# A four-layer kernel on a 256x256x128 image: how layer 1 is loaded, stored and summed

## The chip, the cores and the metric

The kernel runs on one core of a Trainium2 chip. The metric is the device time of one execution in microseconds. The engines of the core are TensorE (PE, with its weight loads shown apart as PEld), VectorE (DVE), ScalarE (ACT), GpSimd (POOL) and SyncE (SP). SP, ACT and POOL can issue DMAs; SP and ACT do it through the hardware queues, POOL through a software queue. All of them are carried out by the core's 16 DMA engines.

## The reference, cut to what matters

The input is x, 256 x 256 positions by 128 channels, in float32. Four layers each add to x what they compute from a group-normalised x. Layer 0 is an attention along rows with a bias between pairs of positions; layers 2 and 3 are not touched by the change. Layer 1 is what the change is about: two sets of 16 planes a and b of 256 x 256, a matrix product of each pair of planes, a normalisation over the 16 channels, and a gate.

```python
def _gn(v, G=32, eps=1e-5):            # per group of 4 channels, over all positions
    ...
def _L1_conv_ref(x, Wa1, ba1, Wa2, ba2, Wb1, bb1, Wb2, bb2, ln2_g, ln2_b, Wg, bg, Wz, bz):
    a = jax.nn.sigmoid((x @ Wa1 + ba1) * (x @ Wa2 + ba2))      # 16 channels
    b = jax.nn.sigmoid((x @ Wb1 + bb1) * (x @ Wb2 + bb2))
    g = jax.nn.sigmoid(x @ Wg + bg)
    z = jnp.einsum('bikc,bkjc->bijc', a, b)                    # one product of planes a channel
    return g * (_ln(z, ln2_g, ln2_b) @ Wz + bz)

x = x + _L0_conv_ref(_gn(x), ...)      # attention
x = x + _L1_conv_ref(_gn(x), ...)
x = x + _L2_conv_ref(_gn(x), ...)
x = x + _L3_conv_ref(_gn(x), ...)
```

## The kernel before

The image is kept in device memory with channels as rows: x1T is x after layer 0 (128 rows of 65536 positions, 32 MB), x2T is x after layer 1. It is worked on in 32 pieces of 2048 positions (SC), 1 MB each; NSC is 32, CK is 512.

Layer 0 first writes the transposed input xT and collects moments; then, in an order of pieces given by a list, it computes the bias of pairs and the sums of squares. Pieces in `held` are resident and are written out by keep(), the others are fetched:

```python
fresh = range(RES - 3, RES)
order = list(range(RES - 3, RES + 4))
for i in range(RES - 3):
    order += [i, RES + 4 + i] if RES + 4 + i < NSC else [i]
# ... in the loop over order:
if s not in held:
    fetch()
    if i > 1:
        keep()
```

The setup of the attention turns the bias (tri) and multiplies it with the row scales, one head at a time, in one DVE instruction:

```python
rsT = eb.tile([P, 2, N], F32, name="p2_rsT", tag="p2_es", bufs=5)
nc.scalar.copy(rsT, pt)
# ...
def turn_pair(h):
    pt = psM.tile([P, 2, N], F32, name="p2i_t", tag="p2_mm")
    turn(pt, tri[:, h, :, :])
    nc.vector.scalar_tensor_tensor(triT[:, h, :, :], pt, toff[:, h : h + 1], rsT, ALU.add, ALU.mult)
```

The attention works on 64 groups of 1024 positions and stores each to x1T on SP's queue. Each half group adds an entry to the statistics (stats1, 128 entries). After it a flag is computed from an aggregate of these statistics (a fallback is taken if something isn't finite), and only then do the folds of layer 1 begin, with a second aggregate of the same statistics (gn_finish):

```python
mv = sb.tile([P, 2], F32, name="chk_mv")
nc.vector.bn_aggr(mv, stats1.rearrange("p n s -> p (n s)"))
# ... flag
again = nc.values_load(flag[0:1, 0:1], min_val=0, max_val=1)
with tc.If(again > 0):
    general_attention(...)
layer0.close()
m1, r1 = gn_finish(stats1, "gn1")
# ... folds of the weights: v1, v2, vb1, vb2, wgf, bgf
```

Layer 1, the a/b stage: each piece is loaded, multiplied with the two sets of weights (a and b side by side: 32 rows for each quarter of the piece, 128 partitions in all), and stored as 32 rows of abD. Eight pieces stay resident for the gate stage.

```python
def store_groups(queue, dst, s, src):
    queue.dma_start(dst[:, s * SC : (s + 1) * SC].rearrange("c (q t) -> q c t", q=4), src)

held = {s: xres.tile([P, SC], F32, name=f"x1_{s}") for s in range(0, NSC, NSC // R1)}   # R1 = 8
for s in range(NSC):
    xt = held[s] if s in held else xsb.tile([P, SC], F32, name="p3_x", tag="xs")        # 3 buffers
    nc.sync.dma_start(xt, x1T[:, ss])
    # ... 8 matmuls into p1 and p2
    s1 = sb.tile([P, CK], F32, name="p3_s1")
    nc.scalar.activation(s1, p1, AF.Identity, bias=vb1)
    nc.vector.scalar_tensor_tensor(s1, p2, vb2, s1, ALU.add, ALU.mult)
    ab = sb.tile([P, CK], F32, name="p3_ab", bufs=10)
    nc.scalar.activation(ab, s1, AF.Sigmoid)
    store_groups(nc.gpsimd, abD, s, ab)
```

The product: 16 pairs of planes, loaded by four, turned, multiplied. The sum and the sum of squares over the channels are kept on POOL, and at the end each plane is scaled with the inverse deviation and stored to znD.

```python
nc.vector.tensor_tensor(Z[:, k, :], pz, base, ALU.subtract)
nc.scalar.activation(sq, Z[:, k, :], AF.Square)
nc.gpsimd.tensor_tensor(s1, s1, Z[:, k, :], ALU.add)
nc.gpsimd.tensor_tensor(s2, s2, sq, ALU.add)
# ... after the last plane:
for i in range(3):
    fetch1(xsb, "xs", 3)                      # pieces for the gate stage
# ... s1 = 1 / sqrt(s2 / 16 - (s1 / 16)^2 + eps)
for q in range(4):
    zq = Z[:, 4 * q : 4 * q + 4, :]
    nc.vector.tensor_tensor(zq, zq, s1.unsqueeze(1).to_broadcast([P, 4, 2 * N]), ALU.mult)
    nc.sync.dma_start(znD[4 * q : 4 * q + 4, :].rearrange("c (p t) -> p c t", p=P), zq)
```

The gate stage takes the pieces once more, with the planes znD in blocks of four pieces, and writes x2T:

```python
zns[b] = sb.tile([P, 4, CK], F32, name="p4_zn", bufs=3)          # fetch_zn(b): 4 loads on SP
# per piece: 4 matmuls with wgf, 2 sigmoids (ACT), 4 matmuls of planes,
# 2 scalar_tensor_tensor (DVE), then
nc.gpsimd.tensor_tensor(xt, xt, gt, ALU.add)
# finish: 4 bn_stats (DVE), store of the piece to x2T on SP; then the next fetch1
# into "xs" (3 buffers) or "xs2" (4 buffers)
```

Of the kernel before, what the change touches and what calls it, by code (L numbers as in the profile page):

```python
# [32 lines left out]
def kernel(ctx: ExitStack, tc: tile.TileContext, a: dict, out: bass.AP):  # L33
# [169 lines left out]
    def gn_groups(mv, name):  # L203
        with tc.tile_pool(name=name + "_ps", bufs=1, space=PSUM) as ps, tc.tile_pool(
# [4 lines left out]
            mean = const.tile([P, 1], F32, name=name + "_mean")  # L209
# [8 lines left out]
            rstd = const.tile([P, 1], F32, name=name + "_rstd")  # L218
# [30 lines left out]
    with tc.tile_pool(name="x0", bufs=1) as xres, tc.tile_pool(name="p0", bufs=3) as sb:  # L249
# [118 lines left out]
        order = list(range(RES - 3, RES + 4))  # L368
        for i in range(RES - 3):
            order += [i, RES + 4 + i] if RES + 4 + i < NSC else [i]  # L370
# [49 lines left out]
        with tc.tile_pool(name="p1", bufs=2) as wk_sb, tc.tile_pool(  # L420
# [9 lines left out]
            with tc.manual_schedule():  # L430
# [5 lines left out]
                for i, s in enumerate(order):  # L436
# [12 lines left out]
                    if s not in held:  # L449
                        fetch()  # L450
                        if i > 1:
                            keep()
# [39 lines left out]
    with tc.tile_pool(name="p2c", bufs=1) as cs:  # L492
        triT = cs.tile([P, NH, 2, N], F32, name="triT")
        with tc.tile_pool(name="p2", bufs=2) as sb, tc.tile_pool(name="p2e", bufs=6) as eb, tc.tile_pool(
# [151 lines left out]
            def close(g, c):  # L646
                x1 = groups[g]["x"]
                nc.vector.bn_stats(stats1[:, g * 2 + c, :], x1[:, c * CK : (c + 1) * CK])
                if c == 1:
                    nc.sync.dma_start(x1T[:, g * GT : (g + 1) * GT], x1)  # L650
                    del groups[g]
# [17 lines left out]

            rb = psS.tile([P, 2, CK], F32, name="p2i_rb", tag="p2_S")  # L670
            for c in range(2):
                nc.tensor.matmul(
                    rb[:, c, :], lhsT=sel[32 * c : 32 * c + 32, 0:1].to_broadcast([32, P]),
                    rhs=rs0[32 * c : 32 * c + 32, :], start=True, stop=True,
                )
            pt = psS.tile([P, 2, N], F32, name="p2i_rs", tag="p2_S")
            for w in range(2):
                for u in range(2):
                    nc.tensor.transpose(
                        pt[:, u, :].rearrange("p (s c w) -> p w c s", c=4, w=2)[:, w],  # L680
                        rs0[:, w * N + u * P : w * N + (u + 1) * P], ident,
                    )
            rsT = eb.tile([P, 2, N], F32, name="p2_rsT", tag="p2_es", bufs=5)
            nc.scalar.copy(rsT, pt)
            tiles(0)
            nc.vector.tensor_tensor(xn, xn, rb.rearrange("p c t -> p (c t)"), ALU.mult)

            def turn_pair(h):
                pt = psM.tile([P, 2, N], F32, name="p2i_t", tag="p2_mm")
                turn(pt, tri[:, h, :, :])  # L690
                nc.vector.scalar_tensor_tensor(triT[:, h, :, :], pt, toff[:, h : h + 1], rsT, ALU.add, ALU.mult)
# [4 lines left out]
            turn_pair(0)  # L696
            turn_pair(1)
            project(0, "q", 0)
            shift(0)
            project(0, "k", 0)  # L700
            shift(1)
            turn_pair(2)
            turn_pair(3)
            shift(2)
            shift(3)
# [6 lines left out]
            for j in range(2 * NG + 5):  # L712
# [55 lines left out]
                if half == 0 and 0 <= g - 2 < NG:  # L768
                    divide(g - 2)
                if half == 1 and g + 2 < NG:  # L770
                    prepare(g + 2)


    flag = const.tile([P, 1], mybir.dt.int32, name="flag")
    with tc.tile_pool(name="chk", bufs=1) as sb, tc.tile_pool(name="chkps", bufs=1, space=PSUM) as ps:
        mv = sb.tile([P, 2], F32, name="chk_mv")
        nc.vector.bn_aggr(mv, stats1.rearrange("p n s -> p (n s)"))
        ok = sb.tile([P, 2], F32, name="chk_ok")
        nc.vector.tensor_scalar(ok, mv, 0.0, 0.0, ALU.mult, ALU.is_equal)
# [4 lines left out]
        nc.vector.tensor_tensor(flag, bad[:, 0:1], bad[:, 1:2], ALU.max)  # L784
    again = nc.values_load(flag[0:1, 0:1], min_val=0, max_val=1)
    with tc.If(again > 0):
# [4 lines left out]
        )  # L791

# [3 lines left out]
    layer0.close()  # L796
    m1, r1 = gn_finish(stats1, "gn1")

    v1 = const.tile([P, 32], F32, name="v1")
    v2 = const.tile([P, 32], F32, name="v2")  # L800
    vb1 = const.tile([P, 1], F32, name="vb1")
    vb2 = const.tile([P, 1], F32, name="vb2")
    wgf = const.tile([P, D], F32, name="wgf")
    bgf = const.tile([P, 1], F32, name="bgf")
    with tc.tile_pool(name="f1ps", bufs=1, space=PSUM) as ps:
        for w, wf_, ub, vb, n in ((u1, v1, ub1, vb1, "1"), (u2, v2, ub2, vb2, "2")):
            nc.vector.tensor_scalar(wf_, w, r1, None, ALU.mult)
            pb = ps.tile([P, 1], F32, name="f1_u" + n)
            for q in range(4):
                nc.tensor.matmul(pb[32 * q : 32 * q + 32, :], lhsT=wf_, rhs=m1, start=True, stop=True)  # L810
            nc.vector.tensor_tensor(vb, ub, pb, ALU.subtract)
        nc.vector.tensor_scalar(wgf, wg1, r1, None, ALU.mult)
        pb = ps.tile([P, 1], F32, name="f1_g")
        nc.tensor.matmul(pb, lhsT=wgf, rhs=m1, start=True, stop=True)
        nc.vector.tensor_tensor(bgf, bg1, pb, ALU.subtract)
    stats2 = new_stats("stats2")
    R1 = 8
    with tc.tile_pool(name="x1", bufs=1) as xres, tc.tile_pool(name="xs1", bufs=3) as xsb:
        held = {s: xres.tile([P, SC], F32, name=f"x1_{s}") for s in range(0, NSC, NSC // R1)}
        with tc.tile_pool(name="p3", bufs=3) as sb, tc.tile_pool(name="p3ps", bufs=3, space=PSUM) as ps:  # L820
            for s in range(NSC):
                ss = slice(s * SC, (s + 1) * SC)
                xt = held[s] if s in held else xsb.tile([P, SC], F32, name="p3_x", tag="xs")
                nc.sync.dma_start(xt, x1T[:, ss])
                p1 = ps.tile([P, CK], F32, name="p3_1")
                p2 = ps.tile([P, CK], F32, name="p3_2")
                for pp, w in ((p1, v1), (p2, v2)):
                    for c in range(4):
# [3 lines left out]
                        )  # L832
# [938 lines left out]
```

## Time and profile before

The kernel takes 3433.33 us (median of 3 runs, 3432.02 to 3438.17). The profiled execution spans 3430.3 us, with a mean granted TensorE clock of 0.955.

| engine | busy us | share |
|---|---|---|
| PE | 3116.2 | 91% |
| DVE | 2317.8 | 68% |
| ACT | 1955.5 | 57% |
| POOL | 1650.9 | 48% |

The stages that the change touches lie in the span as follows. The limits are read from the first and last instructions and transfers of each stage.

| stage | us from the start |
|---|---|
| layer 0 before attention | 0 to 241 |
| setup of the attention | 241 to 262 |
| attention | 262 to 1484 |
| flag, statistics, folds | 1483 to 1499 |
| layer 1: a and b | 1493 to 1618 |
| layer 1: product of planes | 1618 to 1690 |
| layer 1: gate | 1690 to 1871 |
| layers 2 and 3 | 1871 to the end |

A profile is one execution. Its page gives the busy share of each engine in 40 equal slices as a digit in tenths; a table by stage gives the same for stretches that one chooses. The chain of waits is followed back from the last instruction: at each step to what released it, or to the instruction ahead of it on its engine. A line of the chain has the start, the length and what it was: an engine with the name of what it wrote and the line of the kernel, or a DMA with its target and source. In a timeline a line has start, length, engine, line, operation, target, source and, in brackets, the idle time before it and what ended it. A DMA that is not fast enough shows twice: as a chain of DMA lines, and as a DMA share near 1 with no compute engine near its own limit.

### The profile page before, as it was taken

What the parts mean: (1) busy time and instruction counts of PE and PEld (TensorE: products, weight loads), DVE (VectorE), ACT (ScalarE), POOL (GpSimd) and SP (SyncE); (2) the same over time, 40 slices, a digit from 0 to 9 for tenths busy, and PEclk for the clock granted to TensorE, in tenths of its full rate; (3) what the DMA queues carried; (4) which work ended last, traced back from release to release, by engine and by line L of the source; (5) the groups of instructions that cost most, each with busy time, mean ns of one, the idle gap of its engine ahead of it and who ended that gap; (6) DMA issues with size and microseconds to landing.
All of it is one profiled execution on the core that took longest, in us unless ns stands there. A gap on an engine that the chain in (4) does not pass through costs nothing.

```text
span 3430.3 us, 52490 instructions
## 1 busy us (share of the span) xinstructions
PE 3116.2 (91%) x20266; PEld 1646.9 (48%) x20266; DVE 2317.8 (68%) x2635; ACT 1955.5 (57%) x2140; POOL 1650.9 (48%) x914
## 2 busy tenths in 40 slices
PE   5669999999999999954697999999999999959998
PEld 5425555555555555511432344444899533314444
DVE  5627888888888888841497544544555677848876
ACT  3567777777777777722343444543444466736665
POOL 4046777777777777721596000000555344514443
PEclk8889999999999999978898999999999999969999
DMA  9982333333333333269599676865999899847774
GB/s 392 344 296 81 119 108 123 107 119 111 115 118 107 118 109 122 94 244 360 177 337 363 224 291 228 310 239 215 343 350 353 304 336 337 304 165 208 201 206 130
DMA packets 302409, 755.31 MB, mean 220 GB/s; under 512 B 79577, under 2 KB 150139, under 8 KB 252363
## 3 DMA queue, kind: packets, MB, share of 16 engines
q1 hardware_dynamic: 288235, 741.02, 61.3%
q0 software_dynamic: 13920, 10.87, 1.1%
q8 instruction: 162, 2.65, 0.3%
q14 instruction: 92, 0.75, 0.1%
HBM read 464.09 MB, written 287.66 MB: 219 GB/s over the span
## 4 chain that ended last, share of the span: by engine, by line
PE 43%; DMA 8%; DVE 2%; issue 1%; ACT 1%; POOL 1%; SPq 0%; ACTq 0%; POOLq 0%; DVEq 0%
PE p_pm L1063 13%; PE tp_z L1729 7%; PE p_pm L1216 6%; PE p_pm L1451 6%; DMA p_x<-x1T 2%; DMA abD<-p_ab 2%; PE tp_a L1718 2%; PE p_pt L1488 1%; PE p_st L1020 1%; DMA x2T<-p_x 1%; PE p_pg L927 1%; PE p_rz L977 1%; PE p_eb L977 1%; PE p_rk L977 1%; PE p_pp L1344 1%
## 5 line engine op out<-in xcount | busy, mean ns | idle before, releaser
L575 DVE TENSOR_TENSOR p_e<-p_S,triT 128x1024 f32<-128x1024 f32 x512 | 609.2, 1211 | 144.6 <-PE p_S L565 144.6
L585 POOL TENSOR_TENSOR p_es<-p_e 128x1024 f32<-128x1024 f32 x256 | 603.4, 2368 | 125.0 <-issue 66.3
L583 ACT ACTIVATE p_e<-p_e,mbT 128x1024 f32<-128x1024 f32 x512 | 552.1, 1138 | 60.4 <-DVE p_e L575 60.2
L1063 PE MATMUL p_pm<-p_zn,wf 128*128 128x512 f32 x1040 | 451.1, 596 | 1.4 <-DVE p_zn L1080 1.4
L550 PE MATMUL p_mm<-p_xn,w 128*128 128x512 f32 x768 | 406.9, 613 | 0.3 <-DVE p_v L545 0.3
L1063 PEld LDWEIGHTS p_pm<-p_zn,wf 128*128 128x128 f32 x1040 | 197.9, 191 | 255.4 <-issue 248.6
L565 PE MATMUL p_S<-p_q,p_k 32*128 32x256 f32 x4096 | 295.7, 401 | 3.2 <-DVE p_e L575 3.2
L1465 POOL TENSOR_TENSOR p_q<-p_q,p_pb 128x2024 f32<-128x2024 f32 x32 | 144.2, 4505 | 246.8 <-DVE p_pb L1459 246.8
L565 PEld LDWEIGHTS p_S<-p_q,p_k 32*128 32x128 f32 x4096 | 186.2, 184 | 159.2 <-PE p_mm L541 91.7
L1129 POOL DMA_DIRECT2D rs__17885<-rs2D x4 | 2.0, 514 | 534.3 <-PE p_pm L1063 534.3
L1729 PE MATMUL tp_z<-p_B,tp_at 128*128 128x256 f32 x1024 | 250.8, 388 | 2.4 <-DMA p_B<-bD 2.1
L524 POOL TENSOR_TENSOR p_xn<-p_xn,p_rs 128x1024 f32<-128x1024 f32 x63 | 151.3, 2402 | 206.8 <-DMA p_rb<-rzD 119.9
L598 PE MATMUL p_o<-p_e,p_v 128*32 128x256 f32 x4096 | 247.6, 382 | 0.0
L1172 POOL TENSOR_TENSOR k<-k,p_sq 128x512 f32<-128x512 f32 x128 | 163.0, 1274 | 135.5 <-ACT p_sq L1170 135.5
L1282 POOL TENSOR_TENSOR p_x<-p_x,p_g 128x2048 f32<-128x2048 f32 x30 | 136.4, 4546 | 161.0 <-DVE p_g L1269 97.6
L1729 PEld LDWEIGHTS tp_z<-p_B,tp_at 128*128 128x128 f32 x1024 | 185.5, 191 | 25.0 <-issue 2.4
L550 PEld LDWEIGHTS p_mm<-p_xn,w 128*128 128x128 f32 x768 | 126.5, 191 | 105.6 <-issue 89.6
L1171 DVE TENSOR_TENSOR k<-tp_z,k 128x512 f32<-128x512 f32 x128 | 88.6, 692 | 129.1 <-ACT p_sq L1170 129.1
L598 PEld LDWEIGHTS p_o<-p_e,p_v 128*32 128x32 f32 x4096 | 120.0, 109 | 109.3 <-ACT p_g L556 41.5
L1096 DVE SCALAR_TENSOR_TENSOR p_b<-p_pm,b2w,p_b 128x1024 f32<-128x1024 f32 x64 | 82.2, 1284 | 126.0 <-PE p_pm L1063 111.6
L1168 ACT COPY p_K<-tp_z 128x512 f32<-128x512 f32 x128 | 75.0, 586 | 159.9 <-PE tp_z L1729 159.9
L541 PEld LDWEIGHTS p_mm<-w,p_xn 128*128 128x128 f32 x1024 | 134.4, 191 | 61.1 <-issue 60.4
(367 smaller groups left out, 5922.2 us busy)
## 6 DMA issues: line engine op xcount, KB each, us to landing
p_x<-x2T SPq DMA_DIRECT2D x64, 1024.0 KB
p_x<-x1T SPq DMA_DIRECT2D x48, 1024.0 KB
p_x<-in_x_dram SPq DMA_DIRECT2D x32, 1024.0 KB
p_x<-xT SPq DMA_DIRECT2D x64, 512.0 KB
p_rb<-rzD SPq DMA_DIRECT2D x256, 128.0 KB
x1T<-p_x SPq DMA_DIRECT2D x64, 512.0 KB
aD<-p_a SPq DMA_DIRECT2D x32, 1024.0 KB
bD<-p_b SPq DMA_DIRECT2D x32, 1024.0 KB
```

The source lines that it names most:

```text
L524: nc.gpsimd.tensor_tensor(xn, xn, groups[g]["rs"], ALU.mult)
L550: nc.tensor.matmul(pm, lhsT=w, rhs=t["xn"][:, cs_], start=True, stop=True)
L565: nc.tensor.matmul(Ss[h // 2][:, h % 2, u, :], lhsT=t["k"][hp, r * N + u * P : r * N + (u + 1) * P], rhs=t["q"][hp, r * N : (r + 1) * N], ...
L575: nc.vector.tensor_tensor(e[:, :, 2 * p : 2 * p + 2, :].rearrange("p u h n -> p h u n"), Ss[p], triT[:, 2 * p : 2 * p + 2, :, :], ALU.add,)
L583: nc.scalar.activation(e[:, u, :, :], e[:, u, :, :], AF.Exp, bias=mbT[:, u, i : i + 1])
L585: nc.gpsimd.tensor_tensor(es, e[:, 0, :, :], e[:, 1, :, :], ALU.add)
L598: nc.tensor.matmul(t["o"][hp, r % 2, :], lhsT=t["v"][:, r * 2 + u, hp], rhs=e[:, u, h, :], start=(u == 0), stop=(u == 1),)
L1063: nc.tensor.matmul(pm[:, c, :], lhsT=wf2[:, i, :], rhs=zns[s][:, k * CK : (k + 1) * CK], start=True, stop=True)
L1172: nc.gpsimd.tensor_tensor(k2, k2, sq, ALU.add)
L1216: nc.tensor.matmul(pm[:, c, :], lhsT=w, rhs=src[:, k * CK : (k + 1) * CK], start=True, stop=True)
L1451: nc.tensor.matmul(pm[:, 2 * c : 2 * c + 2, :], lhsT=w2c, rhs=src[:, r : r + 2, :], start=True, stop=True)
L1729: nc.tensor.matmul(pz[:, t, :], lhsT=at[:, u, t * P : (t + 1) * P], rhs=Bc[:, u, :], start=(u == 0), stop=(u == 1))
```

## The change

The change rewrites how layer 1 is fed and stored, and a part of layer 0. Its parts:

- Layer 0 before attention: resident and fetched pieces are interleaved from the fourth on, and two resident ones come last. In the setup of the attention the turned bias leaves PSUM through ACT, and DVE multiplies it with the row scales, which it reads from PSUM.
- First pieces: eight pieces of layer 1 get their own space, which comes free while attention drains, and are loaded by SP then. The last two stores of attention go to ACT's queue, so that SP isn't held by them.
- One split aggregation: the first 126 entries of the statistics are aggregated during the drain, the last two after it, and the two parts are merged. The flag and the folds use the same result, and the folds stand before the branch.
- a and b are stored by ACT, on its hardware queue, in place of POOL. Ten pieces stay resident instead of eight, loads run six pieces ahead, and there are eight buffers for a/b instead of ten.
- The product: the plane sum is kept by DVE and the sum of squares by POOL; the fourth of the four last multiplies is done by POOL; two pieces are fetched ahead instead of three.
- The gate: the planes are loaded by ACT, one block ahead, into two buffers instead of three; the pieces have 2 + 3 buffers instead of 3 + 4.

```diff
-        order = list(range(RES - 3, RES + 4))
+        order = list(fresh)
         for i in range(RES - 3):
-            order += [i, RES + 4 + i] if RES + 4 + i < NSC else [i]
+            order += [i, RES + i] if RES + i < NSC - 2 else [i]
+        order += [NSC - 2, NSC - 1]
...
-                        if i > 1:
+                        if i > 2:
                             keep()
...
-                    nc.sync.dma_start(x1T[:, g * GT : (g + 1) * GT], x1)
+                    queue = nc.sync if g < NG - 2 else nc.scalar
+                    queue.dma_start(x1T[:, g * GT : (g + 1) * GT], x1)
...
+            for h in range(NH):
+                pt = psM.tile([P, 2, N], F32, name="p2i_t", tag="p2_mm")
+                turn(pt, tri[:, h, :, :])
+                nc.scalar.activation(triT[:, h, :, :], pt, AF.Identity, bias=toff[:, h : h + 1])
...
+            for h in range(NH):
+                nc.vector.tensor_tensor(triT[:, h, :, :], triT[:, h, :, :], rsT, ALU.mult)
...
+                if j == 2 * NG + 2:
+                    mv_first = gn_part(stats1, 0, 2 * NG - 2, "gn1_a")
...
+    keep1 = list(range(0, NSC, 3))[:10]
+    FIRST = 8
+    for s in keep1[:FIRST]:
+        held1[s] = x1_pool.tile([P, SC], F32, name=f"x1_{s}")
+        load1(s)
+    mv1 = gn_merge(mv_first, gn_part(stats1, 2 * NG - 2, 2 * NG, "gn1_b"), 1.0 - 1.0 / NG, "gn1_mv")
...
-        mv = sb.tile([P, 2], F32, name="chk_mv")
-        nc.vector.bn_aggr(mv, stats1.rearrange("p n s -> p (n s)"))
...
+    fold1("gn1")                                   # the folds, now ahead of the branch
     again = nc.values_load(flag[0:1, 0:1], min_val=0, max_val=1)
...
-    m1, r1 = gn_finish(stats1, "gn1")
...
+            order = keep1[:FIRST] + [s for s in range(NSC) if s not in held]
+            def close3():
+                s, s1 = abs_.pop(0)
+                ab = sb.tile([P, CK], F32, name="p3_ab", bufs=8)
+                nc.scalar.activation(ab, s1, AF.Sigmoid)
+                store_groups(nc.scalar, abD, s, ab)
+            for i in range(FIRST, FIRST + 6):
+                load3(i)
...
-                ab = sb.tile([P, CK], F32, name="p3_ab", bufs=10)
-                nc.scalar.activation(ab, s1, AF.Sigmoid)
-                store_groups(nc.gpsimd, abD, s, ab)
...
-                        nc.gpsimd.tensor_tensor(s1, s1, Z[:, k, :], ALU.add)
+                        nc.vector.tensor_tensor(s1, s1, Z[:, k, :], ALU.add)
                         nc.gpsimd.tensor_tensor(s2, s2, sq, ALU.add)
...
-                nc.vector.tensor_tensor(zq, zq, s1.unsqueeze(1).to_broadcast([P, 4, 2 * N]), ALU.mult)
+                (nc.gpsimd if q == 3 else nc.vector).tensor_tensor(
+                    zq, zq, s1.unsqueeze(1).to_broadcast([P, 4, 2 * N]), ALU.mult
+                )
...
-                zns[b] = sb.tile([P, 4, CK], F32, name="p4_zn", bufs=3)
+                zns[b] = sb.tile([P, 4, CK], F32, name="p4_zn", bufs=2)
                 for c in range(4):
-                    nc.sync.dma_start(
+                    (nc.sync if b == 0 and c % 2 else nc.scalar).dma_start(
...
-                        fetch1(*((xsb, "xs", 3) if len(loaded) % 7 < 3 else (sb, "xs2", 4)))
+                        fetch1(*((xsb, "xs", 2) if len(loaded) % 5 < 2 else (sb, "xs2", 3)))
```

## The prediction

> **What bounds the kernel now.** I read in this order: the busy share by slice, to see where the tensor engine is not the limit; the table by stage; the chain of waits through layer 1; the queues. From the page first:
>
> ```profile
> DMA  9982333333333333269599676865999899847774
> ```
>
> Each digit is a slice of 85.8 us (3430.3 / 40). Slices 18 to 22 (1475 to 1873 us) are layer 1, all that the change rewrites apart from the setup of layer 0. The DMA engines are at 9 there except in slice 18 (6; attention ends in it) and slice 20 (5; 1630 to 1715, the planes' product). The table by stage makes it sharper (columns: stretch, length, busy us and count of PE, weight loads, DVE, ACT, POOL, then granted clock, DMA share, GB/s):
>
> ```profile
> core 0: us, PE busy (x) PEld busy (x) DVE busy (x) ACT busy (x) POOL busy (x), PEclk, DMA share, GB/s
> 1493.00:1618.00 125.00, 65.51 (x534) 18.65 (x534) 26.80 (x43) 43.19 (x67) 22.18 (x32) 0.87 0.96 362
> 1690.00:1871.00 181.00, 156.94 (x508) 59.07 (x508) 157.68 (x197) 72.98 (x66) 145.03 (x32) 0.91 0.98 331
> 1526.00:1545.00 19.00, 12.80 (x112) 3.56 (x104) 5.39 (x8) 8.88 (x14) 4.84 (x7) 1.00 1.01 383
> 1613.50:1615.00 1.50, 0.00 (x0) 0.00 (x0) 0.00 (x0) 0.00 (x0) 0.00 (x0) 0.50 0.40 121
> 1615.50:1616.50 1.00, 0.00 (x0) 0.00 (x0) 0.00 (x0) 0.00 (x0) 0.00 (x0) 0.50 0.24 94
> ```
>
> The a/b stage (1493 to 1618) and the gate stage (1690 to 1871) are bound by transfers: share 0.96 and 0.98, no compute engine above 87%. The last two rows are the tail of the a/b stage, where only stores are left in flight: the share falls to 0.40 and then to 0.24, and 4 of 16 engines is 0.25. So the last store of a and b alone keeps four DMA engines busy, not sixteen.
>
> The chain of waits (start, length, what):
>
> ```profile
> 1551.75 38.05 DMA abD<-p_ab
> ...
> 1609.53 7.99 DMA abD<-p_ab
> 1617.79 5.10 DMA z_A<-abD
> ...
> 1643.38 3.72 PE tp_z L1729 x16
> 1648.29 3.72 PE tp_z L1729 x16
> ...
> 1674.65 8.91 DVE Z L889 x4
> ...
> 1746.65 12.48 DMA p_x<-x1T
> 1759.19 11.05 DMA x2T<-p_x
> ```
>
> In the a/b stage the chain runs through stores of a and b (one took 38.05 us to land in the crowd, the last 7.99); the product starts when the last has landed. The product goes by 4.91 us a pair of planes (1648.29 - 1643.38), PE-bound. In the gate stage loads and stores alternate. The queues from 1490 to 1620 (packets, MB, share of 16 engines over the 130 us):
>
> ```profile
> q1 hardware_dynamic: 5111, 36.85, 71.1%
> q0 software_dynamic: 8704, 8.44, 21.2%
> ...
> abD<-p_ab POOLq DMA_DIRECT2D x32, 256.0 KB, 17.2
> ```
>
> The rate of one DMA engine follows: 36.85 MB / (0.711 x 16 x 130 us) = 24.9 GB/s on the hardware queue, 8.44 / (0.212 x 16 x 130) = 19.1 GB/s on the software queue, which carries exactly the 32 stores of a and b.
>
> [...] The store of a and b goes from 128 partitions to a destination whose slowest dimension is 4[...]. The trace of before agrees for the software queue (0.24 above). For the hardware queue it has one witness, the 4-row stores of the attention, from 600 to 1200 us:
>
> ```profile
> DMA packets 20921, 68.21 MB, mean 114 GB/s; under 512 B 4054, under 2 KB 4559, under 8 KB 20856
> ...
> rzD<-p_rz SPq DMA_DIRECT2D x128, 4.0 KB
> ```
>
> [...] The 96 transfers of 512 KB and about 126 of 128 KB account for 222 x 16 = 3552 of the 4054; the other 502 belong to 128 four-row stores, 3.9 each. [...]
>
> ```profile
> 1667.48 1.74 DVE L882 SCALAR_TENSOR_TENSOR z_s<-z_s 128x512 f32<-128x512 f32 x1 [1.45 <-POOL z_s L877]
> ```
>
> It took 1.74 us beside POOL's last sum (1.26 us from 1667.41); a 128x512 operation of the same kind with an input in PSUM takes 0.75.
>
> **The change, part by part.**
>
> *Layer 0.* Four resident pieces that stood in a row are interleaved, two held ones now come last, and the turned bias is evacuated by ACT before the row scales are known. Loads, stores and matmuls are the same in number. The stage before attention runs at DMA tenths 9, 9, 8; I count +1 us, give or take 4.
>
> *Flag and first loads.* Before, two full aggregations of the statistics ran one after the other, 3.62 us each, and the first load of layer 1 was issued at 1493.3; the first matmul came at 1505.45. Now most of the aggregation is done in the drain, the folds precede the branch, and eight pieces (8 MB) are loaded from about 1466 on. The DMA engines have room: from 1475 to 1493 their share is 0.16. 8 MB at some 380 GB/s is 22 us, so they land by about 1496, and the not-taken branch waits for them; compute and further loads start at about 1498. In itself that takes 8 MB off a transfer-bound stage: 8.4 MB / 362 GB/s = 23 us, and with the earlier start up to 27.
>
> *The stores on ACT's hardware queue.* Work by engine. A 1 MB load lies on 16 engines: 65.5 KB each, 65.5 / 24.9 = 2.63 us. A 256 KB store on four engines is also 65.5 KB each, 2.63 us, but on those four only. [...] these carry, from 1498: 24 loads x 2.63 = 63 us and 32 stores x 2.63 = 84 us, together 147 us. The other twelve carry 63. The stage then ends at 1498 + 147 = 1645, plus 3 us for the last store's start and landing: 1648 instead of 1617.8, **+30 us**. A piece then costs 5.26 us on the hot engines (load and store). PE (1.92 a piece), ACT (0.69 + 0.63) and DVE (0.75) stay hidden under that, and eight buffers of a/b make ACT wait for stores.
>
> *The product.* It is PE-bound at 4.91 us a pair; moving one of two sums of 1.25 us from POOL to DVE (0.7) changes only the end: about -0.6. The normalising multiplies took 8.91 us as four of 2.23 on DVE. The fourth goes to POOL: 2048 columns take POOL 4.51 us (its gate-stage sum of that shape). Both engines read two SBUF inputs[...]: 3 x 2.23 + 4.5 = 11.2, +2.3. Together +2.
>
> *The gate stage.* Its first planes are loaded by two queues: -1. Ten pieces are resident instead of eight, two fewer 1 MB loads in this stage, less one because two rather than three are fetched during the product: 1 MB / 331 GB/s = -3, of which I count -2. It has five buffers instead of seven for pieces and two instead of three for planes.
>
> Sum: 3433.3 + 1 + 30 + 2 - 1 - 2 = 3463 us.
>
> **The rivals.**
>
> *A: the stores spread over 16 engines.* Then the a/b stage has 24 + 8.4 MB = 33.6 MB left at 1498 and needs 33.6 / 0.362 = 93 us: it ends at about 1591, 27 us sooner, and the total is 3433 + 1 - 27 + 2 - 3 = 3406. For it: the change was surely meant so, and the gap in the software rate (19.1 against 24.9 GB/s) goes away. Against it: the 0.24 row[...]. It falls also if ACT's choice of engines rotates. I give it about one in six.
>
> *B: the gate stage turns into latency.* With five buffers a load is issued later, and ACT, which now issues the loads of the planes, may wait in front of its sigmoids. A load or store in this stage took 11 to 12.5 us in the crowd at a pace of 181 / 32 = 5.7 us a piece, so five buffers cover 28 us against load, compute (about 12) and store, some 35. Against it: the ten resident pieces stand between and need no load. Worth +10 to +20: 3475 to 3482.
>
> *C: the multiplies overlap after all.* Then three on DVE (6.7) outlast POOL's 4.5: -2.2 instead of +2.3. It moves the sum by 4 us and cannot decide the sign.
>
> **Range and chances.** The main case is 3463, rival A 3406, B above 3475; weighing A in, I put the time at 3460. The range 3410 to 3482 spans them. For over 2% faster the time would have to be under 3364.7, 69 us less, more than all that the a/b stage can give (its 8 MB and its software tail are some 30 us); for over 2% slower, above 3502, which takes the hot engines and rival B both at full size: 3463 + 20 is still below. So 0.02, 0.94, 0.04.
>
> **What would show it.** Hot engines: from 1500 to 1640 the DMA share falls from 0.96 to about (12 x 63 + 4 x 147) / (16 x 147) = 0.57, with no compute engine taking its place, and the product's first load stands near 1648. ACT's idle time before the sigmoids is then put down to stores of a/b. If the share stays above 0.9 and the product starts near 1591, rival A holds and I am wrong by 55 us. First loads: the first matmul of the stage at about 1498. Multiplies: a DVE multiply of about 6.7 us beside POOL's 4.5, or POOL's ending after 11 us. Gate stage: 178 us at share 0.98 if I am right, 190 or more at a share under 0.92 under rival B. Layer 0: attention begins within 4 us of before.

## The result and the profile after

The changed kernel takes 3484.81 us (median of 4 runs, 3478.42 to 3496.74) against 3434.27 before (median of 4). The ratio is 1.015, with a 95% interval of 1.0119 to 1.0181. That is 50.5 us more, where 3460 was predicted with a range of 3410 to 3482: the time lies 2.8 us above the range. The profiled execution spans 3479.4 us, 49.1 more than that of before.

The busy share of the DMA engines by slice, from the page of the changed kernel:

```profile
DMA  9872333333333333375598686775999899846674
```

The slices of layer 1 (18 to 22, counted from 1) read 7, 5, 5, 9, 8 where they read 6, 9, 5, 9, 9: the a/b stage, in slices 18 and 19, no longer fills the engines. The table by stage (columns as in the prediction; rows: a/b stage, its tail, gate stage):

```profile
1500.00:1640.00 140.00, 74.87 (x512) 17.10 (x506) 24.03 (x32) 40.08 (x65) 0.00 (x0) 0.79 0.65 248
1638.00:1646.00 8.00, 0.00 (x0) 0.00 (x0) 0.00 (x0) 0.63 (x1) 0.00 (x0) 0.50 0.26 102
1725.00:1910.00 185.00, 155.83 (x504) 57.45 (x504) 154.98 (x193) 71.78 (x65) 144.94 (x32) 0.92 0.91 318
```

The a/b stage has a share of 0.65, and no compute engine is near its limit. In the tail several stores are still in flight (ACT issued the last of them at 1638.8, and at 102 GB/s more than four stores are left to move until 1650), and yet the share is 0.26: four engines at the 24.9 GB/s worked out in the prediction make 100. Before, the share fell to 0.24 only with the very last store. The queues from 1490 to 1660 (packets, MB, share of 16 engines) show that the software queue's 8.44 MB are now on a second hardware queue, at 8.91 MB / (0.134 x 16 x 170 us) = 24.4 GB/s for each engine at work:

```profile
q1 hardware_dynamic: 5586, 32.47, 50.2%
q10 hardware_dynamic: 4368, 8.91, 13.4%
...
abD<-p_ab ACTq DMA_DIRECT2D x32, 256.0 KB
```

The chain of waits of this profile can be followed back to 1916 us only, so layer 1 is read from its timeline. The tensor engine (start, length, operation, idle time before and what ended it):

```profile
1655.68 3.33 PE L1765 MATMUL tp_a<-ident,z_A 128*128 128x128 f32 x14 [27.65 <-DMA z_A<-abD]
...
1730.32 3.88 PE L981 MATMUL p_pz<-p_zn,wzc 16*128 16x512 f32 x8 [28.09 <-DMA p_zn<-znD]
```

The product's first turn stood at 1623.02 before, the first product with normalised planes at 1692.95. So 32.7 us are lost by the first row and 37.4 by the second. The length of each stage, from its first matmul to the next stage's first, worked out from the starts in the traces, shows where the 49 us are. Two limits are others: the last stage of layer 2 is counted over 25 of its 32 pieces (2741.4 to 2978.2 before, 2780.8 to 3017.7 changed; the rest goes to the rows around it), and layer 3 up to the last matmul.

| stretch, us | before | changed | difference |
|---|---|---|---|
| start to attention | 262.0 | 259.7 | -2.3 |
| attention, flag, folds | 1243.5 | 1240.1 | -3.4 |
| a/b stage to first turn of the product | 117.6 | 155.9 | +38.3 |
| product to first product with planes | 69.9 | 74.6 | +4.7 |
| gate stage to the next statistics | 175.1 | 182.3 | +7.2 |
| layer 2 up to its last stage | 873.4 | 868.2 | -5.2 |
| last stage of layer 2 | 236.8 | 236.9 | +0.1 |
| layer 3 | 442.8 | 452.3 | +9.5 |

Between product and gate, the multiplies and the stores of the planes look like this in the changed kernel, on DVE, POOL and SP's queue in turn:

```profile
1706.42 8.79 DVE L934 TENSOR_TENSOR Z<-Z,z_s 128x2048 f32<-128x2048 f32 x2
```

```profile
1706.46 6.60 POOL L934 TENSOR_TENSOR Z<-Z,z_s 128x2048 f32<-128x2048 f32 x1 [5.41 <-DVE z_s L931]
```

```profile
1713.09 4.71 SPq L937 DMA_DIRECT2D znD<-Z  x4
```

The first two DVE multiplies took 8.79 us where four took 8.90 before; POOL's took 6.60, and 4.5 for the same shape in the gate stage. And the first store is issued at 1713.09, when POOL is done, though the first DVE multiply took 2.3 us as ever and ended at 1708.7; before, the four stores were issued from 1677.02 on, 2.4 us after the multiplies began. In the gate stage, ACT and its queue:

```profile
1773.44 9.31 ACTq L950 DMA_DIRECT2D p_zn<-znD  x4
1782.86 2.12 ACT L976 ACTIVATE p_g<-p_pg,bgf 128x1024 f32<-128x1024 f32 x2 [8.36 <-DMA p_zn<-znD]
```

ACT needs 9.31 us to issue four loads, because it waits for earlier transfers, and its sigmoids stand behind them. Four such waits add up to 26.0 us, of which the tensor engine felt 12.6. POOL, whose sum makes the piece that is stored, shows what that costs. When nothing stops it, its sums of 4.5 us follow each other with 0.2 us between them; behind ACT's four stops it has six longer gaps, 15.7 us together. The first of them:

```profile
1786.56 4.53 POOL L990 TENSOR_TENSOR x<-x,p_g 128x2048 f32<-128x2048 f32 x1 [4.55 <-DVE p_g L987]
```

Where no such stop falls, the pace is that of before, 4.75 us a piece, though the DMA share is lower (first row before, second row changed):

```profile
1710.00:1750.00 40.00, 40.00 (x138) 15.06 (x135) 40.00 (x51) 18.29 (x18) 38.26 (x9) 1.00 0.99 321
1745.00:1780.00 35.00, 34.12 (x121) 12.56 (x120) 34.75 (x45) 14.36 (x13) 33.39 (x8) 1.00 0.86 303
```

DVE is busy 40.00 of 40 us before and 34.75 of 35 changed, and PE and POOL nearly so. The 87% that the prediction read for the whole stage before is an average over this even part and the two ends.

### The profile page after: what moved, and what is told of

Read it like the earlier page. It is cut to its first block, busy times and chain, and to the rows that moved or that the text cites. A ratio compares the mean times of both kernels' runs of the same rounds, so it can differ in the third digit from the quotient of the medians.

```text
span 3479.4 us, 52442 instructions
## 1 busy us (share of the span) xinstructions
PE 3128.4 (90%) x20266; PEld 1649.7 (47%) x20266; DVE 2327.8 (67%) x2655; ACT 1954.8 (56%) x2143; POOL 1617.4 (46%) x868
## 5 line engine op out<-in xcount | busy, mean ns | idle before, releaser
L1219 POOL TENSOR_TENSOR k<-k,p_sq 128x512 f32<-128x512 f32 x128 | 163.0, 1273 | 135.2 <-ACT p_sq L1217 135.2
```

The lines of the kernel that those rows point to most:

```text
L1219: nc.gpsimd.tensor_tensor(k2, k2, sq, ALU.add)
```

## The experiments

Times are medians; ratios are to the kernel before, measured in the same session, with their 95% intervals. The last four columns are lengths in the one profiled run, which for 128 rows is the lowest of 20 (3418.1 us) and in the row "three mends, gate supply" 11 us above the median. "The loop" in the last column is explained with the fifth experiment.

| run | us | ratio to before | a/b stage | product to planes | gate | last stage of layer 2 |
|---|---|---|---|---|---|---|
| changed kernel | 3484.8 | 1.0119 to 1.0181 | 155.9 | 74.6 | 182.3 | 236.9 |
| stores on POOL's queue | 3462.1 | 1.0041 to 1.0088 | 113.8 | 74.0 | 183.9 | 272.2 (loop) |
| before, stores on ACT's | 3492.7 | 1.0148 to 1.0182 | 169.6 | 69.5 | 178.6 | 236.9 |
| stores in quarters | 3474.8 | 1.0087 to 1.0132 | 135.2 | 74.7 | 181.3 | 248.5 (loop) |
| 128 rows | 3448.7 | 1.0005 to 1.0046 | 98.0 | 73.6 | 182.3 | 236.9 |
| planes on SP's queue | 3501.6 | 1.0151 to 1.0213 | 155.0 | 73.3 | 190.6 | 260.5 (loop) |
| multiplies on DVE | 3481.2 | 1.0117 to 1.0159 | 156.6 | 70.0 | 181.6 | 236.9 |
| gate supply of before | 3476.3 | 1.0101 to 1.0141 | 158.5 | 73.6 | 177.0 | 236.9 |
| POOL's queue, layer 2 swapped | 3433.4 | 0.9979 to 1.0006 | 109.8 | 74.3 | 181.0 | 236.9 |
| before, layer 2 swapped | 3437.1 | 0.9994 to 1.0018 | 114.8 | 69.8 | 174.4 | 236.9 |
| three mends | 3420.3 | 0.9928 to 0.9964 | 97.7 | 70.5 | 182.6 | 236.9 |
| three mends, gate supply | 3412.1 | 0.9910 to 0.9951 | 99.7 | 68.8 | 179.4 | 236.9 |
| changed, layer 2 swapped | 3482.3 | 1.0113 to 1.0146 | 155.4 | 74.0 | 182.9 | 236.9 |

### 1. The stores back on POOL's queue

```diff
-                store_groups(nc.scalar, abD, s, ab)
+                store_groups(nc.gpsimd, abD, s, ab)
```

> The changed kernel with one word undone: a and b go back to POOL's software queue. Theory (ACT's hardware queue puts all 32 stores on the same four DMA engines): [...]the DMA share of the a/b stage returns to 0.9 or more, the product's first turn starts at about 1600 us instead of 1655.7, and the kernel takes about 3430 us, 55 less than the changed kernel. Rival 1 (the stage is long because loads run six ahead, in another order, with fewer buffers): the product still starts after 1645 and the time stays above 3475. Rival 2 (ACT is held up by issuing stores): like the theory here; the run with quarters tells it apart.

The a/b stage fell from 155.9 to 113.8 us and the first turn came at 1607.8, so the rival that blames loading order and buffers is out. The first loads give less than was counted on, though: against before, on the same queue, the stage is 3.8 us shorter and the first turn 15.2 us sooner. But the time was 3462, not 3430: up to the end of layer 1 this run stands 2.4 us below before, and then loses some 36 us in a stage of layer 2 that neither kernel changes. The fifth experiment takes that up.

### 2. Before, with the stores alone moved to ACT

```diff
-                store_groups(nc.gpsimd, abD, s, ab)
+                store_groups(nc.scalar, abD, s, ab)
```

> The kernel before, with only the stores of a and b moved from POOL's queue to ACT's. Theory: the four engines carry 32 loads and 32 stores of 2.63 us each from 1502 on, 168 us, so the product's planes are loaded from about 1673 instead of 1617.8 and the kernel takes about 3488 us, 54 more than before. Rival 1 (the loading order is at fault, not the queue): no more than 5 us of difference from before, 3430 to 3440.

The time was 3492.7, 54.8 more than before in that session (3437.8), with 54 expected. The a/b stage of this run:

```profile
1502.00:1665.00 163.00, 74.27 (x512) 16.60 (x503) 23.89 (x32) 42.82 (x65) 0.00 (x0) 0.76 0.66 251
```

It ran for 164 us where the sum for four fixed engines is 32 x 2.63 + 32 x 2.63 = 168, with a mean share of 0.66; that sum makes (12 x 84 + 4 x 168) / (16 x 168) = 0.63. If the four engines moved from store to store, each engine would carry 84 + 32 x 0.66 = 105 us (0.66 is a quarter of 2.63) and the stage would end 60 us sooner. One word of the program costs 55 us. That the four are the same for every store is read from these sums, 164 us measured against 168 and 105; which four they are, no view shows.

### 3. The same queue, other shapes: quarters, and 128 rows

```diff
-                store_groups(nc.scalar, abD, s, ab)
+                for q in range(4):
+                    nc.scalar.dma_start(abD[:, s * SC + q * CK : s * SC + (q + 1) * CK], ab[32 * q : 32 * q + 32, :])
```

> The changed kernel with each store of a and b cut into four, one for each quarter, still on ACT's queue: 32 rows to 32 rows, so each may lie on 16 engines. Theory (four fixed engines): 33.6 MB are left at 1500 and need 93 us, the product's first turn starts at about 1600, the time is about 3428. Rival 2 (what costs is ACT waiting in front of its stores): ACT now issues 128 stores instead of 32, so the stage is as long or longer, first turn at 1655 or later, time 3485 or more.

The first turn came at 1637.3, between the two that were expected: the stage took 135.2 us, 21 less than in the changed kernel and 37 more than the 128 rows below. ACT's timeline in this run shows the rest:

```profile
1547.67 2.83 ACTq L862 DMA_DIRECT2D abD<-p_ab  x4
1550.56 0.69 ACT L881 ACTIVATE p_s<-p,vb 128x512 f32<-128x512 f32 x1 [2.91 <-DMA abD<-p_ab]
```

and so do the waits of SP's queue (what waited, for what, us in total, times, longest):

```profile
SPq L855 <- DMA abD<-p_ab: 33.4, 11, 6.8
```

Four issues a piece cost ACT 1.7 to 4.2 us in the stretch that I read, and SP's loads waited 33 us for stores. So this miss mixed two things: more engines (their number is estimated from the packets, below) and four times as many transfers. The next run keeps the number of stores.

```diff
-    abD = rows("abD", 32)
+    abD = dram.tile([P, NSC * CK + PAD], F32, name="abD")[:, 0 : NSC * CK]    # row: quarter, channel
-                store_groups(nc.scalar, abD, s, ab)
+                nc.scalar.dma_start(abD[:, s * CK : (s + 1) * CK], ab)
...
-                nc.sync.dma_start(A, abD[4 * q : 4 * q + 4, :].rearrange("c (p t) -> p c t", p=P))
+                for r in range(4):
+                    nc.sync.dma_start(
+                        A.rearrange("(s r) c t -> r s c t", r=4)[r],
+                        abD[32 * r + 4 * q : 32 * r + 4 * q + 4, :].rearrange("c (s t) -> s c t", t=CK))
```

> The changed kernel with a and b laid out in device memory as 128 rows (quarter and channel), so that one store of a piece, still on ACT's queue and still one for each piece, has 128 rows on both sides and may lie on 16 engines; the planes are then loaded in four parts each. This separates the number of engines from the number of stores, which the run with quarters changed too. Theory (four engines are the limit): share of the a/b stage 0.9 or more, the product's first turn at about 1600 us (1655.7 in the changed kernel), and about 50 us less there. Rival (ACT's queue and its waits are the limit, whatever the shape): first turn at 1640 or later.

```profile
1493.00:1586.00 93.00, 62.81 (x512) 16.92 (x504) 24.50 (x33) 40.10 (x65) 0.00 (x0) 0.90 0.97 387
```

The share is 0.97 at 387 GB/s, the stage is 98.0 us long, and the first turn comes at 1590.7, 65 us ahead of the changed kernel (7 of them arose ahead of the stage). The queue is the same, the stores are as many and as large; in this stage only the rows on the far side differ, 128 where the slowest dimension was 4. The tensor engine waits for loads there, no longer for ACT (34.1 us in the changed kernel):

```profile
PE p L871 <- DMA p_x<-x1T: 19.9, 13, 4.4
```

The packets of ACT's queue give the number of engines another way. First the kernel before with its stores on ACT's queue (1495 to 1672 us), then the 128 rows (1490 to 1600):

```profile
q10 hardware_dynamic: 4224, 8.39, 12.4%
q10 hardware_dynamic: 4608, 8.39, 19.8%
```

8.39 MB in packets of 2 KB are 4096; the rest is 128 and 512, so 4 and 16 for each of the 32 stores. A transfer of 1 MB has 16 such small packets as well: 816 under 512 B for 51 of them, in the changed kernel from 2830 to 2990, where the queue's share is 93.6%. The run with quarters has 6288 packets on ACT's queue (8.92 MB, 1490 to 1640) where the changed kernel has 4368 (8.91 MB, 1490 to 1660); the 1920 more are 128 x 16 less 32 x 4, so its small stores have 16 each. That there is one such packet for each engine is an estimate: it fits the shares, 0.26 x 16 = 4.2 in the changed kernel's tail and 0.97 x 16 = 15.5 with 128 rows.

The total is another matter: of this kernel's 20 runs five lie at 3418 to 3427 and fifteen at 3440 to 3464. The profiled one is the lowest, so what holds the fifteen up is in no trace.

### 4. The hand-over to the gate stage, and the gate stage

All four multiplies on DVE:

```diff
-                (nc.gpsimd if q == 3 else nc.vector).tensor_tensor(
+                nc.vector.tensor_tensor(
```

> The changed kernel with the fourth normalising multiply back on DVE. Theory ([...]the stores of the planes wait for POOL's multiply and bunch up): from the reciprocal to the first product with planes 22 to 23 us instead of 27.3. Rival (the bunching comes from the two queues that load the planes): still 26 or more. The total is expected within the spread of the changed kernel, so the stage decides and not the time.

```profile
1707.85 8.90 DVE L934 TENSOR_TENSOR Z<-Z,z_s 128x2048 f32<-128x2048 f32 x4
```

```profile
1710.17 6.97 SPq L937 DMA_DIRECT2D znD<-Z  x4
```

```profile
1727.33 4.02 PE L981 MATMUL p_pz<-p_zn,wzc 16*128 16x512 f32 x8 [23.66 <-ACT p_g L976]
```

The stores start 2.3 us after the first multiply again, and from the reciprocal (1704.46) to the first product with planes it is 22.9 us, against 27.3 in the changed kernel. The stretch is back at 70.0 us against 69.9 before, with the planes still on two queues. Its parts are the same to 0.4 us in all fourteen profiles of this case. The first store is issued 10.1 us after the reciprocal begins where POOL has a multiply, and 5.7 where it has none; the first planes are loaded 12.6 to 12.8 us after that store in every case; the first product follows 4.4 to 4.7 us later with two queues, and 3.3 to 3.4 with SP's alone. So the 4.4 us by which the first store is late are the loss, and the two queues cost 1.1 us instead of bringing 1. Why a store of planes that DVE finished waits for POOL is open.

The planes on SP's queue:

```diff
-                    (nc.sync if b == 0 and c % 2 else nc.scalar).dma_start(
+                    nc.sync.dma_start(
```

> The changed kernel with all planes of the gate stage loaded by SP's queue instead of ACT's, two plane buffers as in the change. Theory (ACT stands in front of its sigmoids while its load waits for an earlier transfer: 26 us in four waits): the waits are gone, from the first product with planes to the last aggregate 171 us as before instead of 178.5, time about 3477. Rival (five piece buffers and two plane buffers are too few): the stage stays at 178 and the time at 3485.

A clear miss: the gate stage grew from 182.3 to 190.6 us (the expectations of this run and the next count to the aggregate, 3.8 us less). ACT had no such wait left, but POOL's gaps are now at other places (26 us beyond the usual 0.2, against 19 in the changed kernel and 10 before), and SP's queue waited for stores ahead of a load:

```profile
SPq L891 <- DMA x2T<-p_x: 81.6, 13, 10.6
```

With two plane buffers, one block ahead, the loads of the planes now stand behind such waits. That this is what costs is argued, not shown: the next run has 76.5 us of the same wait and a short stage. Nor does the run clear ACT's queue, behind whose stops the changed kernel loses its time; it shows that moving the loads alone is no cure. The supply of before in the changed kernel:

```diff
-    keep1 = list(range(0, NSC, 3))[:10]
+    keep1 = list(range(0, NSC, 3))[:8]
-                zns[b] = sb.tile([P, 4, CK], F32, name="p4_zn", bufs=2)
+                zns[b] = sb.tile([P, 4, CK], F32, name="p4_zn", bufs=3)     # two blocks ahead, on SP's queue
-                        fetch1(*((xsb, "xs", 2) if len(loaded) % 5 < 2 else (sb, "xs2", 3)))
+                        fetch1(*((xsb, "xs", 3) if len(loaded) % 7 < 3 else (sb, "xs2", 4)))
```

> The changed kernel with the gate stage's supply of before: eight resident pieces, 3 + 4 buffers for pieces, three for planes, two blocks ahead, all on SP's queue. Theory (too few buffers make the stage wait for transfers; the queue alone does not, as the planes on SP's queue gave no gain): from the first product with planes to the aggregate of the next layer's statistics 171 us as before instead of 178.5. Rival (what is lost comes from the late and bunched start of the stage): still 177 or more.

```profile
1728.00:1900.00 172.00, 156.99 (x504) 58.82 (x504) 152.06 (x191) 69.03 (x62) 144.97 (x32) 0.94 0.98 341
```

The share is back at 0.98 and the stage at 177.0 us, 5.3 of the 7.2 us lost, though two more pieces are loaded. All profiles say the same: the stage takes 174.4 to 179.4 us in the five with this supply and 181.0 to 183.9 in the eight with that of the change. The late start explains next to nothing of it: with the multiplies on DVE the hand-over was mended and the gate stage stayed at 181.6. The run takes back four things at once, resident pieces, piece buffers, plane buffers and the queue of the planes; three plane buffers, two blocks ahead, with the loads still on ACT's queue would tell the last two apart, and were not tried.

### 5. Where layers 2 and 3 come in

In the first experiment layer 2's last stage took 272.2 us instead of 236.8 (over all its pieces the loss is 36.7 us). Its waits on SP's queue, from 2830 to 2990:

```profile
SPq L1186 <- DMA x3T<-p_x: 134.5, 13, 10.7
```

and a stretch of SP's timeline at the beginning of the trouble:

```profile
2792.10 0.32 SPq L1186 DMA_DIRECT2D p_x<-x2T  x1
2793.33 0.32 SPq L1281 DMA_DIRECT2D x3T<-p_x  x1
...
2803.51 0.32 SPq L1186 DMA_DIRECT2D p_x<-x2T  x1
2803.92 0.39 SPq L1281 DMA_DIRECT2D x3T<-p_x  x1
...
2815.19 0.32 SPq L1186 DMA_DIRECT2D p_x<-x2T  x1
2815.61 0.38 SPq L1281 DMA_DIRECT2D x3T<-p_x  x1
```

In each round SP issues a load that may start only when the store of the round before has landed, and behind it the next store. At first the store follows the load by 1.2 us, and later by 0.4: it had been ready, and stood behind the load. From then on a round lasts 11.7 us (2803.51 to 2815.19), of which 11.3 pass from the store (2803.92) to the load that waits for it to land, instead of 9.4 (17 pieces in the 160 us of the run below), and no slack is won back. The edit puts the load behind the store:

```diff
         for s in range(NSC):
             load7k(s + 3)
-            load7x(s + 5, ...)
...
                 if s:
                     finish7(s - 1)
+            load7x(s + 5, ...)
```

> The run with a and b on POOL's queue, with one more edit in layer 2, which the change does not touch: the next load of a piece is issued after the store of the piece before, not ahead of it. In that run layer 2's last stage took 36 us longer than before: SP stood 134 us of 160 in front of that load, waiting for a store to land, while the next store stood behind it. Theory (the stage falls into a loop of store, load, store once a store lands late): the stage takes what it took before, the kernel about 3435 instead of 3462, with a smaller spread. Rival (something that the change does earlier slows the transfers there): no gain, 3455 to 3468.

```profile
2792.00:2952.00 160.00, 160.00 (x546) 59.43 (x545) 122.74 (x103) 107.18 (x102) 77.23 (x17) 1.00 0.89 335
```

The tensor engine is busy all the time, the stage takes 236.9 us, and the kernel 3433.4 (3426.99 to 3442.38 over 12 runs) instead of 3462.1 (3452.64 to 3467.70 over 4). What SP waits for now is POOL, whose sum makes the piece to be stored. The same edit in the kernel before and in the changed one:

> The kernel before, with only the order of load and store in layer 2's last stage turned round. In its profile that stage is not in the loop, and none of its runs is as far above the lowest as the kernels on the base of the change are. Theory (before hardly ever falls into the loop): the same time as before within 5 us, median 3433 to 3440. Rival (before falls into it late in many runs, which makes its spread of 18 us): 5 to 10 us faster, and a spread under 10 us.

Before did not gain: 3437.1 against 3436.1, over 14 runs that spread by 24 us, so its spread is not the loop.

> The changed kernel with only layer 2's load put after its store. It tells how much of the changed kernel's loss is not layer 1 at all. Theory (the changed kernel's profile has no loop, but its slower runs do: they spread from 3478 to 3497): median about 3480, 5 less than the changed kernel, all runs under 3487. Rival (the spread comes from layer 3, whose length moves by 10 us between profiles of all kernels): median 3485, spread as before the edit.

The changed kernel stood at 3482.3 (3477.36 to 3484.90, 4 runs) instead of 3484.8 (3478.42 to 3496.74). The two high runs are gone, but with four runs each this is a hint and no more. Why the kernels on the base of the change fall into the loop and before hardly does is open; no run was made for it. Layer 3 moves by itself: 449 to 460 us in the profiles of the changed kernel and of all experiments, against 442.8 in that of before, whose profile is thus a short one.

### 6. What beats both

Three mends together (128 rows on ACT's queue, multiplies on DVE, layer 2 swapped), and with the gate supply of before as a fourth:

> The changed kernel with three mends: a and b as 128 rows on ACT's queue, the fourth multiply on DVE, and layer 2's load after its store; the gate stage's supply as in the change. Theory (the three costs add up): first turn of the product at about 1592, from there to the first product with planes 70, the gate stage 181, layer 2's last stage 237, total about 3414 in every run, 25 less than before, with no runs above 3430. Rival (the layer 2 loop comes back in another form, or the gate stage gives the gain back): 3425 or more.

> As the run with three mends, and also the gate stage's supply of before (eight resident pieces, 3 + 4 and 3 buffers, planes on SP's queue). Theory (the gate stage takes 177 instead of 181 to 182 when it has more buffers): about 3409, 4 to 5 less than with the three mends. Rival (two pieces more to load in a stage at the limit of the transfers cost what the buffers bring): the same as with three mends, 3412 to 3418.

The three mends took 3420.3 us, a ratio of 0.9946 (0.9928 to 0.9964), and the four 3412.1, 0.9931 (0.9910 to 0.9951). The stages came within 3 us of what was expected (97.7, 70.5 and 182.6; then 99.7, 68.8 and 179.4). The total of the first did not: 3414 was expected, with no run above 3430, and one of nine took 3431.2. In its profile the first turn came at 1601.8 instead of 1592, because the a/b stage began 11 us later than in the profile of the 128 rows; layer 0 ahead of it is the same code in both. The gain of the gate supply is 3 us in the stage; the two intervals overlap, so as a difference of totals it isn't shown. So what is left of the change is worth 24 us (3436.1 to 3412.1) once its stores reach all engines and its side effects are undone. Without the swap in layer 2 only five of the 20 runs with 128 rows came under 3430, so it seems to be needed to keep the gain, though it gives the kernel before nothing.

## Why the prediction was wrong, point by point

**The a/b stage: right.** The prediction had the product start near 1648, 30 us late; its planes were issued at 1650.3, and its first turn was 32.7 us late. The loss is shown from both sides: alone in the kernel before it costs 54.8 us, and 128 rows on the same queue bring the stage from 155.9 to 98.0. That the four engines are the same for every store was an estimate, with which the sums of the second experiment agree; why a store of this shape lies on four, no run shows. The share was 0.65 where 0.57 was said. Rival A's number, 27 us sooner, is what the 128 rows reach (32 us); its "24 + 8.4 MB" should read 25.2 + 8.4, and the 33.6 is right.

**Layer 0, flag and first loads: right in kind, the gain too large.** Attention began 2.3 us sooner, not 1 later, within the 255 to 262 us that all profiles spread over; the first matmul of the a/b stage came at 1499.8, where 1498 was said. "Up to 27" us for the loads ahead is not borne out: with the rest of the change in this stage but the same queue as before, the first turn came 15.2 (or, between the two kernels with layer 2 swapped, 5.8) us sooner on POOL's queue and 14.9 on ACT's.

**The product: right, but cut off too early.** "3 x 2.23 + 4.5 = 11.2" came as 10.99 us on DVE beside 6.60 on POOL:

```profile
1706.42 10.99 DVE L934 TENSOR_TENSOR Z<-Z,z_s 128x2048 f32<-128x2048 f32 x3
```

Of DVE's three, one took 6.58 us and the others 2.28 and 2.29; POOL's 6.60 stands against 4.5 for that shape in the gate stage. That the two would take turns was an estimate; these times agree with it, and what makes the engines wait is not shown. But the end of the multiplies is not what the next stage waits for. The first store of the planes waited for POOL's multiply (+4.4), and the two queues cost 1.1 us where "-1" was counted; the product itself came 0.9 us sooner. So the stretch lost 4.7 us where +2 and -1 were in the sum.

**The gate stage: the step that failed.** "1 MB / 331 GB/s = -3, of which I count -2" took the stage as bound by the amount of data. It was +7.2. In the even part of the stage the pace is 4.75 us a piece at a DMA share of 0.99 and of 0.86 alike, with DVE busy all the time, so less data could shorten little beyond its ends; what could lengthen it was a stop, and ACT's four stops for the loads of the planes are followed by 15.7 us of gaps on POOL. Rival B had this ("may wait in front of its sigmoids") and was given +10 to +20; the effect is real and smaller. Its sign came by half: the share was under 0.92 (0.91), the length short of 190 us. The supply of before takes back 5.3 of the 7.2; which of its four parts does it is open, and moving the planes to SP's queue alone made it worse.

**Layers 2 and 3: left out of the sum.** They were put at no change. In the profile they come to +4.4 (-5.2, +0.1, +9.5). No effect of the change is shown by that: the profile of before is the odd one in both large terms, and the two other profiles on its base have 450 us for layer 3, where those on the base of the change have 449 to 460. But the loop of layer 2 can add some 36 us to a kernel of this family, and the upper end of 3482 had no room for what the untouched layers do by themselves.

Together, against the 3463 of the sum, the profiled run at 3481.3 is 18 us higher: about 9 in the gate stage, 4 at the hand-over, 4 in layers 2 and 3, 2 in the a/b stage, less 1 because the profiled run of before was a short one. The chance of 0.94 was put on a time within 2%, and it came so, at 1.5%.

## What to carry to other kernels

Ask of every transfer how many DMA engines it lies on, and sum the work of the fullest engine, not of all (168 us against 105 in the second experiment, where 164 were measured). A DMA share stuck at 0.25 in a tail was the sign here (0.26 with stores of slowest dimension 4 alone in flight), and stores with 32 or 128 rows on the far side had 16 small packets each instead of 4. Read what bounds a stage in its even part and not from its average, and when buffers are taken from it or loads given to an engine that also computes, look for the stops that this brings. And in a queue that issues in order, put a store that is ready ahead of a load that waits for an earlier store (236.9 us instead of 272.2 for layer 2's last stage).

## What the runs showed that I had not expected

A store on 16 engines of a hardware queue beats the software queue by more than its rate: 98.0 us for the stage against 113.8 and 109.8 with POOL's stores. The rates of 24.9 and 19.1 GB/s account for 6.4 us of the difference (8.39 MB on 16 engines). Nor are POOL's stores held to the same four engines, by an estimate from the first experiment: from 1490 to 1640 they took 20.5% of 16 engines' time, which is 82% of four, beside loads at 61.0% of all, and 143% doesn't fit on an engine. Why the rest is lost is not shown. Four small stores in place of one lose much of what the wider spread gains (135.2 against 98.0). And a stage at 100% of the tensor engine can drop by a fifth in pace, from 9.4 to 11.7 us a piece, and stay there, without any change in its own code.
